# A decoder layer on one core: ScalarE copies products out of PSUM, GpSimd's queue takes late stores, scores and values are put side by side, and round 0 loads by use

## The chip, the cores and the metric

The kernel runs on one core of a Trainium2 chip. TensorE (PE) multiplies matrices into PSUM, VectorE (DVE), ScalarE (ACT) and GpSimd (POOL) work on tiles, and DMAs move data between SBUF and DRAM. DMAs are issued by SyncE (SP), by ACT and, after the change, by POOL; each issues its own instructions in order. The metric is the device time of one execution in microseconds (us), the median of three runs.

## The reference

One decoder layer, with layer normalization behind each of its three parts. `x` is 8 x 512 x 512. In the first part, attention runs over the axis of length 8, for each of the 512 columns by itself, with 16 heads of 32 and relative positions. In the second, each of 8 batches attends from its 512 positions to 512 context vectors of 1024 features, with 8 heads of 64 and a mask. The third is a feed-forward part of width 2048, whose hidden values and second weight are rounded to an 8-bit float.

```python
qkv = x @ in_proj_weight.T + in_proj_bias
ac = einsum('tbhd,sbhd->bhts', q + r_w_bias, k)
bd = rel_shift(einsum('tbhd,rhd->bhtr', q + r_r_bias, p))[..., :t]
ctx = einsum('bhts,sbhd->tbhd', softmax((ac + bd) * scale), v)
x = layernorm(x + ctx @ out_proj_weight.T + out_proj_bias)
...
k, v = split((ctx_2048 @ W_src.T + b_src) * mask)
q = (x @ W_tgt.T + b_tgt) * mask
u = softmax(where(mask == 0, -inf, q k^T / 8)) v
x = layernorm(x + concat([x, u]) @ W_out.T + b_out)
...
h = float_quantize(relu(x @ w1.T + b1), 4, 3)
x = layernorm(x + float_quantize(h @ float_quantize(w2, 4, 3).T + bq, 5, 10))
```

## The kernel before

**Stage one** computes the first part. The 512 columns are cut into four blocks `j` of 128, and each block has eight positions `t`. PE projects queries (`queries_of`, part 0 of `project`, line 224), keys and values from `xt`; the keys and values are copied to SBUF by ACT (lines 244 and 294), and DVE adds the bias to the queries out of PSUM (line 253). DVE multiplies queries with keys and reduces (`pq`, lines 257 and 266: 2.3 us each), weighs the values with the softmax (`weigh`, lines 321 to 337, into `ao`), PE transposes `ao` (`turn_out`), ACT copies the result to `aoT`, and PE multiplies it with the output weight (`put_out`, line 354). DVE adds this to the residual `r` out of PSUM (line 370) and takes the statistics; behind every fourth position comes a square root on ACT (`sd_a`, line 106), four normalizations, and four stores to `x1d` from ACT's queue (line 376). The projections share two PSUM banks (`ps_mm`), the output product has one (`ps_o`).

Beside this runs a filling of PE's time: `context_work` projects the context of batches 0 to 5 to keys and values (products `px`, `py`, `pz`, line 694), `project_context` does the same for batch 6, one piece of 16 matmuls for each of four key blocks (`psk`) and four value blocks (`psv`). ACT evicts each piece to a tile `st` and stores it to `kd` or `vd` from its own queue (lines 179 and 193).

In this stage the order of PE's instructions is that in which the program writes them. A small planner writes it: `slot` gives each position a length (11.2 for scores, 12.4 for values), `must` places what has to come, and `fill` puts context products between. The other engines' order is left to the framework's scheduler.

**Stage two** goes through rounds `t` = 0 to 7, one for a batch. Here the order of PE, DVE, ACT and SP is the order of the program. A round has units `u`: for each of four pairs of heads `c`, two units of two query blocks. A score unit (`scores`, line 1112, `s`) multiplies queries `qT` with keys `kT`; DVE adds the mask and finds the maximum (`nmax`, line 1127), ACT takes the exponential (line 1137), DVE divides (line 1152) and transposes 32 x 32 blocks (line 1160, `pb`). Behind a pair's second unit `move_blocks` issues 16 DMAs that move the blocks to where their transpose has them (`pT`, line 1176); in round 0 half of them are on ACT's queue. `pT` has one buffer, so the moves of a pair follow the values product of the pair before. The values product (`attend`, line 1213, `av`) multiplies `v` with `pT`. The values of batches 0 to 5 are loaded raw and turned by DVE (`raw`, `turn_v`).

Dense work is woven between: in round 0 the `project_context` of batch 7 (eight pieces, with `w_src` and `ct7`; two of them in round 1), later the output projection of the round before (`output_of`: `px` on `x1T`, `pu` on `u`, lines 1248 and 1260), the second feed-forward product of two rounds before (`finish`, line 1417, `fin` and `o`), the queries of the next round (`psq`, line 1091), and the first feed-forward product (`hidden_of`, line 1328, `hx`, `hy`, `hz`) in a form with seven block products, whose weight slabs `w1r` are loaded by `load_w1` into the memory that `w_src` has until then.

`weave` merges the two lists. An attention step comes when its gap is used up and when as many dense steps are behind it as it needs; the gap that follows is its weight x the dense cost left / the weights left. `attention_of` makes the list: in rounds 1 to 7 the odd units from 3 on are a score step of weight 0.5 and then a values step of weight 0.5, which needs `projected`, the end of `output_of`. Each step goes through `run`, which first issues due loads (`later`, counted down in steps) and due moves, and then earns credit (0.7 of the step's cost, 1.3 in round 0) for side work on DVE and ACT: `urgent` (the normalization of `x2`) before `side` (exponentials, divisions, transposes, turns, output stores).

At the start of round 0 SP is given `x1T(1)` (four DMAs), the row `bxo` and `x1(0)` at once, ahead of the dense steps; the stores of batch 7's pieces are put on `later` and issued one step behind. After the normalized `x2` is turned, SP stores it (`x2d`, four DMAs, line 1007) and loads it back whole (`x2T`, line 1014).

Of the kernel before, what the change touches and what calls it, by code (L numbers as in the profile page):

```python
# [9 lines left out]
F32 = mybir.dt.float32  # L10
# [3 lines left out]
ALU = mybir.AluOpType  # L14
# [3 lines left out]
P = 128  # L18
E = 512
EC = E // P  # L20

T, NB, H1, D1 = 8, 512, 16, 32
NJ = NB // P
# [15 lines left out]
R_BQ, R_RW, R_BO, R_BXO, R_B2 = range(5)  # L39
# [3 lines left out]
def decoder_layer(  # L43
# [22 lines left out]
    nc = tc.nc  # L66
# [27 lines left out]
    def load_row(pool, r, name):  # L94
        tl = pool.tile([P, E], F32, name=name)
        nc.sync.dma_start(tl, rows[r].partition_broadcast(P))
        return tl
# [60 lines left out]

    big = ctx.enter_context(tc.tile_pool(name="big", bufs=1))

    def project_context(t, w, ct_of, ps_pool, ps_tag, st_pool, st_tag, store):

        def keys(o):
            ps = ps_pool.tile([P, S], F32, tag=ps_tag, name=f"psk{t}_{o}")
            for f in range(FC):
                nc.tensor.matmul(  # L170
                    ps,
                    lhsT=w[0][f][:, o * P : (o + 1) * P],
                    rhs=ct_of(f),
                    start=(f == 0),
                    stop=(f == FC - 1),
                )
            st = st_pool.tile([P, S], F32, tag=st_tag, name=f"kst{t}_{o}")
            nc.scalar.activation(st, ps, AF.Identity, bias=col(C_BK + o))
            store(lambda: nc.scalar.dma_start(kd[t][:, o, :], st))

        def values(s):
            ps = ps_pool.tile([P, E], F32, tag=ps_tag, name=f"psv{t}_{s}")
            for f in range(FC):
                nc.tensor.matmul(  # L184
                    ps,
                    lhsT=ct_of(f)[:, s * P : (s + 1) * P],
                    rhs=w[1][f],
                    start=(f == 0),
                    stop=(f == FC - 1),
                )  # L190
            st = st_pool.tile([P, E], F32, tag=st_tag, name=f"vst{t}_{s}")
            nc.scalar.activation(st, ps, AF.Copy, scale=maskcol[:, t, s : s + 1])
            store(lambda: nc.scalar.dma_start(vd[t][:, s, :], st))

        return [lambda o=o: keys(o) for o in range(EC)] + [
            lambda s=s: values(s) for s in range(ST)
        ]

    with ExitStack() as ph:
# [46 lines left out]
        def queries_of(j, t):  # L246


            if t == 0:
                sc[j] = kvp.tile([P, T, P], F32, tag="sc", name=f"sc{j}")  # L250
            ps = project(xts[j, t], 0, f"q{j}_{t}")
            qw = qp.tile([P, E], F32, tag="qw", name=f"qw{j}_{t}")
            nc.vector.tensor_tensor(qw, ps, bqw, ALU.add)  # L253
            for g in range(2):
                fs = slice(g * HW, (g + 1) * HW)
                pr = prp.tile([P, HH, T, D1], F32, tag="pr", name=f"pq{j}_{t}_{g}")
                nc.vector.tensor_tensor(  # L257
                    pr,
                    qw[:, fs]
                    .rearrange("p (h d) -> p h d", d=D1)  # L260
                    .unsqueeze(2)
                    .to_broadcast([P, HH, T, D1]),
                    k_all[j][:, :, fs].rearrange("p s (h d) -> p h s d", d=D1),
                    ALU.mult,
                )
                nc.vector.tensor_reduce(  # L266
                    sc[j][:, t, g * HH * T : (g + 1) * HH * T],
                    pr.rearrange("p h s d -> p (h s) d"),
                    AX.X,
                    ALU.add,  # L270
                )
# [79 lines left out]
        def put_out(j, t):  # L351
            po = ps_o.tile([P, E], F32, tag="po", name=f"po{j}_{t}")
            for c in range(EC):
                nc.tensor.matmul(  # L354
                    po,
                    lhsT=aoT[t][:, c * P : (c + 1) * P],
                    rhs=w_o[:, c, :],
                    start=(c == 0),
                    stop=(c == EC - 1),
                )  # L360
            r = rp.tile([P, E], F32, tag="r", name=f"r{j}_{t}")
            n0 = t * NB + j * P
            nc.sync.dma_start(r, x[n0 : n0 + P, :])
            nc.gpsimd.tensor_tensor(r, r, bo, ALU.add)
            if t % 4 == 0:
                normed["mv"] = sm.tile([P, 4, 2], F32, tag="mv1", name=f"mva{j}_{t}")
                normed["r"] = []
            mvs, rts = normed["mv"], normed["r"]
            rts.append(r)
            nc.vector.tensor_tensor(r, po, r, ALU.add)  # L370
            stats_of(sm, mvs[:, t % 4, :], r, f"a{j}_{t}")
            if t % 4 == 3:
                rs = rstd_of(sm, mvs, 4, f"a{j}_{t}")
                for i in range(4):
                    normalize(rts[i], rts[i], mvs, rs, i)
                    nc.scalar.dma_start(x1d[t - 3 + i][j], rts[i])

# [419 lines left out]
        def last_but_one():  # L799
            for f in range(FC):  # L800
                ct6.append(xtp.tile([P, S], F32, tag="xt", name=f"ct6{f}"))
                nc.sync.dma_start(ct6[f], ctxT[T - 2, f * P : (f + 1) * P, :])
            return project_context(
                T - 2, w6, lambda f: ct6[f], ps_kv, "kv", kst, "st", lambda f: f()
            )

        filling.append(context_work())
# [82 lines left out]
    with ExitStack() as ph:  # L890
# [45 lines left out]
        def run(cost, step):  # L936

            nonlocal credit
            move()
            credit += pace * cost  # L940
            while credit > 0 and (urgent or side):
                _, work, f = (urgent or side).pop(0)
                credit -= work
                f()
            credit = min(credit, 0.0)
            step()
# [21 lines left out]
        def load_x1(t):  # L968
            x1[t] = qx.tile([P, NJ, E], F32, tag="x1", bufs=2, name=f"x1{t}")
            nc.sync.dma_start(x1[t], x1d[t].rearrange("j p e -> p j e"))  # L970
# [14 lines left out]
        def load_x1T(t):  # L985
            x1T[t] = x1Ts[:, t % 2]
            load_blocks(x1T[t], x1d[t])
# [475 lines left out]
        def of(cost, f, *a):  # L1463
            return [(cost, lambda: f(*a))]
# [34 lines left out]
        def attention_of(t, projected, queried):  # L1499

            steps = []
            last = t + 1 == T
            behind = 2 if t == 0 else 1
            for u in range(1, 2 * EC + (0 if last else 1)):
                n = units[t * 2 * EC + u]
                need = queried if u == 2 * EC else 0
                values = u > 2 * behind and (u % 2 == 1 or (t == 0 and u == 2 * EC))
                weight = 0.5 if values else 1.0  # L1510
                score = (2.0, need, lambda n=n: scores(*n), weight)
                if not values:
                    steps.append(score)
                    continue
                f = lambda c=u // 2 - behind: attend_next(t, c)

                weight = 2.2 if last and u == 2 * EC - 1 else 0.5
                value = (3.8, projected, f, weight)
                steps += [value, score] if t == 0 else [score, value]
            return steps  # L1520

        def output_of(t):
# [11 lines left out]
        with tc.manual_schedule(engines={ET.PE, ET.DVE, ET.Activation, ET.SP}):  # L1534
# [30 lines left out]
            for t in range(T):  # L1565
# [5 lines left out]
                asked = [of(3.6, queries, t + 1, o, mq) for o in range(EC) if t + 1 < T]  # L1571
                asked = sum(asked, [])
                if t == 0:
                    load_x1T(1)
                    bxo = load_row(wb, R_BXO, "bxo")
                    load_x1(0)

                    pieces = project_context(
                        T - 1,
# [3 lines left out]
                        "b",  # L1583
                        sp,
                        "pe",
                        lambda f: later.append([1, f]),
                    )
                    steps = sum([of(7.2, piece) for piece in pieces[:-2]], []) + asked

                    behind = {  # L1590
                        1: of(0.0, convert, 0) + of(0.0, cast_b2),
                        3: of(0.0, convert, 1) + of(0.0, turn_v_soon, 1),
                        4: of(0.0, turn_x1, 1),
                    }
# [3 lines left out]
                else:  # L1598
# [12 lines left out]
                    sums = [of(0.0, sum_x2, t - 1, i) for i in range(4)]  # L1611
                    if t == 1:
                        dense += x1_ahead + after + done[0] + of(0.0, load_x2T, 0)
                        dense += done[1]
                        for i, part in enumerate(((0, 0), (1, 0), (0, 1))):
                            asked[2 * i + 1 : 2 * i + 1] = of(0.0, load_w1, *part)
                    elif t < T - 1:
                        dense += x1_ahead + done[0] + after
                        dense += done[1] + of(0.0, load_x2T, t - 1)
                    else:  # L1620
                        dense += after + done[0] + done[1]
                        for j in range(2):
                            dense += of(0.9, turn_late_x2, t - 1, j)
# [129 lines left out]
```

## Time and profile before

| what | us |
|---|---|
| median of three runs (lowest to highest) | 2048.33 (2047.96 to 2048.45) |
| the profiled execution | 2051.27 |
| its span | 2049.0 |
| PE busy in the span | 2001.7 |
| stage one, to about 867: PE, DVE, ACT, POOL busy | 849.5, 756.5, 117.5, 122.8 |
| 867 to 1066 (round 0, start of round 1): PE, DVE, ACT busy | 182.2, 135.5, 53.5 |
| one of the repeating rounds (136.4): PE, DVE, ACT busy | 135.5, 96.1, 53.1 |

The page gives busy time by engine. In the list of waits a line names the engine, its instruction and source line, what ended the wait, and then the total, the number and the longest of such waits in us. A timeline line has start and length in us, engine, source line, operation, what is written and read, the shape, how many instructions were merged, and in brackets the idle time before it and its cause. `SPq` and `ACTq` are DMA issues in SP's and ACT's order. In the windows the granted clock of TensorE is given as a share: 1.00 is full speed.

### The profile page before, as it was taken

How to read it: one execution, taken by the hardware profiler on the slowest of the kernel's cores; microseconds unless marked ns; L12 is line 12 of the kernel's file. 1: busy time of each engine (PE TensorE's matmuls, PEld its weight loads, DVE VectorE, ACT ScalarE, POOL GpSimd, SP SyncE). 2: the span in 40 equal slices, each digit the busy share in tenths (PEclk: the TensorE clock that was granted, in tenths of full speed). 3: DMA queues.
4: the chain of work that ended last, by engine and by line, in shares of the span. 5: the costliest groups of instructions: out<-in, count | busy, mean ns of one | idle time of the engine just before them, and what ended most of it. 6: DMA issues, size and time to landing. Idle time of an engine off the chain costs nothing.

```text
span 2049.0 us, 19491 instructions
## 1 busy us (share of the span) xinstructions
PE 2001.7 (98%) x6552; PEld 1040.1 (51%) x6552; DVE 1524.0 (74%) x2409; ACT 547.3 (27%) x1194; POOL 214.7 (10%) x211
## 2 busy tenths in 40 slices
PE   9999999999999999998999999999999999999998
PEld 4544444444444444443347456465474564655666
DVE  4999999999999979348675685775856857657343
ACT  2111101110111011123235244253352442534322
POOL 0040012012102120011001001002010010000000
PEclk9999999999999999999999999999999999999999
DMA  6635235342242541497677566676775666753711
GB/s 222 235 103 212 75 121 197 110 159 79 77 166 76 186 164 72 106 291 195 147 204 214 127 166 219 117 223 163 148 215 120 168 218 133 211 154 93 230 47 66
DMA packets 247075, 319.37 MB, mean 156 GB/s; under 512 B 85056, under 2 KB 140352, under 8 KB 242880
## 3 DMA queue, kind: packets, MB, share of 16 engines
q1 hardware_dynamic: 227040, 283.22, 48.9%
q10 hardware_dynamic: 19936, 34.91, 5.1%
q8 instruction: 52, 0.85, 0.2%
q14 instruction: 47, 0.39, 0.1%
HBM read 188.03 MB, written 62.91 MB: 122 GB/s over the span
## 4 chain that ended last, share of the span: by engine, by line
PE 70%; DVE 22%; issue 3%; DMA 2%; SPq 1%; ACT 1%; POOL 0%; ACTq 0%; DVEq 0%
PE hx L1328 11%; PE pox L1260 6%; PE hz L1328 5%; PE pox L1248 5%; PE s L1112 5%; PE av L1213 5%; PE px L694 5%; PE po L354 4%; DVE sc L266 4%; DVE pq L257 3%; PE ps_q L224 3%; PE psv L184 3%; PE o L1417 3%; PE hy L1328 3%; PE psq L1091 3%
## 5 line engine op out<-in xcount | busy, mean ns | idle before, releaser
L1137 ACT ACTIVATE pe<-pe,nmax 128x512 f32<-128x512 f32 x256 | 182.7, 715 | 265.5 <-DVE nmax L1127 236.1
L1127 DVE CUSTOM_DVE_ANT_0 pe<-s,mb 128x512 f32<-128x512 f32 x256 | 162.6, 683 | 27.7 <-PE s L1112 26.9
L1160 DVE STREAM_TRANSPOSE pb<-pe 128x512 f32<-128x512 f32 x256 | 161.7, 681 | 2.4 <-DMA pT<-pb 2.4
L321 DVE TENSOR_TENSOR pv<-v,sc 128x2048 f32<-128x2048 f32 x64 | 147.0, 2298 | 7.4 <-ACT v L294 5.6
L257 DVE TENSOR_TENSOR pq<-qw,k 128x2048 f32<-128x2048 f32 x64 | 151.1, 2361 | 1.2
L266 DVE TENSOR_REDUCE sc<-pq 128x64 f32<-128x2048 f32 x64 | 145.9, 2280 | 1.1
L1112 PE MATMUL s<-kT,qTx 64*128 64x512 f32 x512 | 130.1, 624 | 9.3 <-DMA kT<-kd 5.7
L354 PE MATMUL po<-w_o,aoT 128*128 128x512 f32 x256 | 117.6, 603 | 5.4 <-DVE r L370 5.4
L1213 PE MATMUL av<-pT,vx 128*64 128x512 f32 x512 | 118.6, 606 | 2.9 <-DMA pT<-pb 2.9
L1328 PE MATMUL hx<-x2T,w1r 128*128 128x256 f32 x512 | 118.6, 382 | 2.0 <-ACT hs L1350 2.0
L1091 PE MATMUL psq<-x1Ts,w_tgt 128*128 128x512 f32 x256 | 115.7, 609 | 4.9 <-DVE x1Ts L983 4.9
L224 PE MATMUL ps_k<-w_in,xt 128*128 128x512 f32 x256 | 116.0, 606 | 4.6 <-DMA xt<-in_xT_dram 4.6
L224 PE MATMUL ps_q<-w_in,xt 128*128 128x512 f32 x256 | 117.0, 600 | 2.7 <-DVE qw L253 2.7
L1328 PE MATMUL hx<-x2s,w1r 128*128 128x256 f32 x512 | 118.6, 382 | 0.8 <-DVE hs L1356 0.8
L1356 DVE TENSOR_TENSOR hs<-hz,hs 128x512 f32<-128x512 f32 x32 | 22.1, 692 | 130.0 <-PE hz L1328 128.3
L1152 DVE TENSOR_SCALAR pe<-pe,rden 128x512 f32<-128x512 f32 x256 | 114.8, 491 | 4.5
L1260 PE MATMUL pox<-w_xo,uT 128*128 128x512 f32 x256 | 115.0, 598 | 0.0
L224 PE MATMUL ps_v<-w_in,xt 128*128 128x512 f32 x256 | 114.4, 593 | 0.1
L1248 PE MATMUL pox<-w_xo,x1Ts 128*128 128x512 f32 x256 | 114.0, 593 | 0.0
L1417 PE MATMUL o<-w2q,hq 128*128 128x512 fp8e4 x512 | 113.6, 379 | 0.0
L1328 PEld LDWEIGHTS hx<-x2s,w1r 128*128 128x128 f32 x512 | 96.0, 190 | 25.1 <-DVE nmax L1127 4.5
L1328 PEld LDWEIGHTS hx<-x2T,w1r 128*128 128x128 f32 x512 | 97.8, 192 | 18.1 <-ACT hs L1350 2.4
(169 smaller groups left out, 2859.7 us busy)
## 6 DMA issues: line engine op xcount, KB each, us to landing
pT<-pb SPq DMA_DIRECT2D x480, 128.0 KB, 2.4
w1r<-w1d SPq DMA_DIRECT2D x32, 1024.0 KB, 6.6
w1r<-w1d SPq DMA_DIRECT2D x32, 768.0 KB, 4.6
ch<-in_ctxT_dram SPq DMA_DIRECT2D x24, 512.0 KB, 6.1
td<-tx SPq DMA_DIRECT2D x12, 768.0 KB, 4.9
tx<-td SPq DMA_DIRECT2D x12, 768.0 KB, 7.5
r<-in_x_dram SPq DMA_DIRECT2D x32, 256.0 KB, 4.1
x1d<-r ACTq DMA_DIRECT2D x32, 256.0 KB, 2.5
```

What stands on the lines that cost most here:

```text
L224: nc.tensor.matmul(ps, lhsT=xt[:, e, :], rhs=w_in[:, e, part * E : (part + 1) * E], start=(e == 0), stop=(e == EC - 1),)
L257: nc.vector.tensor_tensor(pr, qw[:, fs] .rearrange("p (h d) -> p h d", d=D1) .unsqueeze(2) .to_broadcast([P, HH, T, D1]), k_all[j][:, :, f ...
L266: nc.vector.tensor_reduce(sc[j][:, t, g * HH * T : (g + 1) * HH * T], pr.rearrange("p h s d -> p (h s) d"), AX.X, ALU.add,)
L354: nc.tensor.matmul(po, lhsT=aoT[t][:, c * P : (c + 1) * P], rhs=w_o[:, c, :], start=(c == 0), stop=(c == EC - 1),)
L1091: nc.tensor.matmul(ps, lhsT=w_tgt[:, e, o * P : (o + 1) * P], rhs=x1T[t][:, e, :], start=(e == 0), stop=(e == EC - 1),)
L1112: nc.tensor.matmul(ps[:, h, :], lhsT=qT[t, c][half[h], j * P : (j + 1) * P], rhs=kT[t, c][half[h], :], start=True, stop=True,)
L1137: nc.scalar.activation(pe, pe, AF.Exp, bias=nmax[:, h : h + 1], scale=-1.0, accum_out=den[:, h : h + 1],)
L1213: nc.tensor.matmul(av[half[h], :], lhsT=v[t, c][:, s, half[h]], rhs=pT[t, c][:, :, :, s, h].rearrange("p g i q -> p (g i) q"), start=(s == 0),
L1248: nc.tensor.matmul(po, lhsT=x1T[t][:, e, j * P : (j + 1) * P], rhs=w_xo[:, e, :], start=(e == 0), stop=False,)
L1260: nc.tensor.matmul(po, lhsT=uT[t][:, e, j * P : (j + 1) * P], rhs=w_xo[:, EC + e, :], start=False, stop=(e == EC - 1),)
L1328: nc.tensor.matmul(banks[g, name][:, i], lhsT=w[:, f, i * P : (i + 1) * P], rhs=b[:, f], start=start and f + i == 0, stop=f == 1, skip_gro ...
L1417: nc.tensor.matmul(po, lhsT=rows_of_j, rhs=w2q[:, c, :], start=(c == 0), stop=(c == HC - 1),)
```

## The change

Five edits are made together.

- In `queries_of` and `put_out` ACT copies the product from PSUM to SBUF (to `qw`, and over `aoT[t]`, which the product has read), and DVE adds from SBUF.
- `project_context` issues its stores from POOL's queue, for both batches, and at once; the delay for batch 7 goes. The last four stores of `x1d` (block 3, positions 4 to 7) are also issued by POOL.
- In rounds 1 to 6 the odd units from 3 on are one step of weight 1.0, which holds the scores and, through a `run` of its own, the values product; it needs what either needed.
- In round 0 `x1T(1)` is loaded behind the first dense step, and `bxo` and `x1(0)` behind the third.
- In round 1 `load_w1(0, 0)` goes ahead of the transposes of `x1T` and the queries; the two that follow go one step later among the queries.

```diff
             st = st_pool.tile([P, S], F32, tag=st_tag, name=f"kst{t}_{o}")
             nc.scalar.activation(st, ps, AF.Identity, bias=col(C_BK + o))
-            store(lambda: nc.scalar.dma_start(kd[t][:, o, :], st))
+            nc.gpsimd.dma_start(kd[t][:, o, :], st)
...
             nc.scalar.activation(st, ps, AF.Copy, scale=maskcol[:, t, s : s + 1])
-            store(lambda: nc.scalar.dma_start(vd[t][:, s, :], st))
+            nc.gpsimd.dma_start(vd[t][:, s, :], st)
...
             qw = qp.tile([P, E], F32, tag="qw", name=f"qw{j}_{t}")
-            nc.vector.tensor_tensor(qw, ps, bqw, ALU.add)
+            nc.scalar.copy(qw, ps)
+            nc.vector.tensor_tensor(qw, qw, bqw, ALU.add)
...
-            nc.vector.tensor_tensor(r, po, r, ALU.add)
+            nc.scalar.copy(aoT[t], po)
+            nc.vector.tensor_tensor(r, aoT[t], r, ALU.add)
...
-                    nc.scalar.dma_start(x1d[t - 3 + i][j], rts[i])
+                    queue = nc.gpsimd if j == NJ - 1 and t == T - 1 else nc.scalar
+                    queue.dma_start(x1d[t - 3 + i][j], rts[i])
...
-                value = (3.8, projected, f, weight)
-                steps += [value, score] if t == 0 else [score, value]
+                if t == 0 or last:
+                    value = (3.8, projected, f, weight)
+                    steps += [value, score] if t == 0 else [score, value]
+                    continue
+
+                def both(n=n, f=f):
+                    scores(*n)
+                    run(3.8, f)
+
+                steps.append((2.0, max(need, projected), both, 1.0))
...
-                    load_x1T(1)
-                    bxo = load_row(wb, R_BXO, "bxo")
-                    load_x1(0)
+                    bxo = wb.tile([P, E], F32, name="bxo")
+
+                    def load_rows():
+                        nc.sync.dma_start(bxo, rows[R_BXO].partition_broadcast(P))
+                        load_x1(0)
...
-                        lambda f: later.append([1, f]),
...
                     behind = {
+                        0: of(0.0, load_x1T, 1),
                         1: of(0.0, convert, 0) + of(0.0, cast_b2),
+                        2: of(0.0, load_rows),
...
-                        dense += done[1]
-                        for i, part in enumerate(((0, 0), (1, 0), (0, 1))):
-                            asked[2 * i + 1 : 2 * i + 1] = of(0.0, load_w1, *part)
+                        dense += done[1] + of(0.0, load_w1, 0, 0)
+                        for i, part in enumerate(((1, 0), (0, 1))):
+                            asked[2 * i + 2 : 2 * i + 2] = of(0.0, load_w1, *part)
```

More of the change, by code (lines that the diff above doesn't have):

```diff
@@ L159, in decoder_layer, with project_context @@
     big = ctx.enter_context(tc.tile_pool(name="big", bufs=1))
-    def project_context(t, w, ct_of, ps_pool, ps_tag, st_pool, st_tag, store):
+    def project_context(t, w, ct_of, ps_pool, ps_tag, st_pool, st_tag):
         def keys(o):
@@ L803, in last_but_one @@
             return project_context(
-                T - 2, w6, lambda f: ct6[f], ps_kv, "kv", kst, "st", lambda f: f()
+                T - 2, w6, lambda f: ct6[f], ps_kv, "kv", kst, "st"
             )
```

## The prediction

> **What bounds the kernel now.** I read the table of busy time first, then PE's waits, then short windows around the long waits, and last the timeline of one repeating round.
>
> ```profile
> span 2049.0 us, 19491 instructions
> PE 2001.7 (98%) x6552; PEld 1040.1 (51%) x6552; DVE 1524.0 (74%) x2409; ACT 547.3 (27%) x1194; POOL 214.7 (10%) x211
> ```
>
> PE is idle for 47.3 us only, and the change takes no matmul away. So it can win PE's idle time, the slow clock behind it, and the cost of switching between kinds of matmul; nothing else. The list of PE's waits says where the idle time lies:
>
> ```profile
> PE s L1112 <- DMA kT<-kd: 5.7, 1, 5.7
> PE po L354 <- DVE r L370: 5.4, 2, 4.4
> PE psq L1091 <- DVE x1Ts L983: 4.9, 1, 4.9
> PE s L1112 <- DVE nmax L1127: 3.6, 4, 0.9
> PE hy L1328 <- DMA w1r<-w1d: 3.5, 1, 3.5
> PE av L1213 <- DMA pT<-pb: 2.9, 1, 2.9
> PE ps_q L224 <- DVE qw L253: 2.7, 1, 2.7
> ```
>
> The change aims at four of these lines: po, ps_q, s on kT, hy on w1r. Windows cut just behind the ends of such waits show a second price (columns: PE, PEld, DVE, ACT, POOL busy, then the granted clock):
>
> ```profile
> 425.60:432.00 6.40, 6.31 (x12) 2.93 (x13) 4.12 (x7) 0.00 (x0) 0.00 (x0) 0.62 0.94 350
> 490.80:496.10 5.30, 5.27 (x9) 2.25 (x10) 5.30 (x5) 0.21 (x1) 0.00 (x0) 0.68 0.00 0
> 930.20:937.00 6.80, 6.76 (x13) 2.67 (x14) 4.40 (x8) 0.61 (x2) 1.48 (x2) 0.60 0.87 218
> 1199.00:1203.00 4.00, 3.11 (x12) 1.28 (x12) 3.89 (x11) 2.08 (x6) 0.00 (x0) 1.00 0.94 204
> ```
>
> After waits of 4.43, 2.72 and 5.74 us the clock is 0.60 to 0.68 for some 5 to 7 us; after one of 0.89 us it stays 1.00. A long wait thus costs 1.8 to 2.9 us more.
>
> In the second stage I read round 2 (PE, then SP's DMA queue):
>
> ```profile
> 1163.80 1.99 PE L1112 MATMUL s<-kT,qTx 64*128 64x512 f32 x8
> 1165.72 7.08 PE L1417 MATMUL o<-w2q,hq 128*128 128x512 fp8e4 x32
> 1172.73 3.65 PE L1213 MATMUL av<-pT,vx 128*64 128x512 f32 x16
> ...
> 1201.20 1.13 PE L1112 MATMUL s<-kT,qTx 64*128 64x512 f32 x4 [0.89 <-DVE nmax L1127]
> ...
> 1209.36 3.65 PE L1213 MATMUL av<-pT,vx 128*64 128x512 f32 x16
> ```
>
> ```profile
> 1180.23 3.54 SPq L1007 DMA_DIRECT2D x2d<-x2T  x4
> 1187.42 0.38 SPq L1014 DMA_DIRECT2D x2T<-x2d  x1
> 1194.52 10.26 SPq L1176 DMA_DIRECT2D pT<-pb  x16
> ```
>
> The values product `av` needs the block transposes' DMAs `pT`. For the second pair of heads these end on SP at 1204.8; with 2.4 us to landing they are there at 1207, and `av` starts at 1209.4: only 2 us to spare.
>
> **The change part by part.**
>
> *ScalarE copies (`queries_of`, `put_out`).* 64 copies are added, at 586 ns each (the same copy of `k`, `v`, `aoT`): 37.5 us on ACT, busy 117 us of the first stage's 867. DVE's 64 additions stay; they take 676 and 684 ns from PSUM now, and 688 to 692 with both inputs in SBUF (`tx`, `x`): +0.8 us, hidden where DVE waits for PE. The gain is that PE's bank is free after ACT's copy. At 421.1 to 425.7 PE waited 4.43 us for `po`; with ACT free, the `aoT` and `po` copies follow one another and leave about 0.4: 4.0 gained, and 2.4 of slow clock (the `po` group took 6.04 us, usually 3.60). Next late is DVE: the two transposes of `ao` after it have 4.4 and 3.0 us of slack now, and DVE itself comes 2.3 us earlier; I give back 1.2. The `ps_q` wait is worth 2.7 and 1.8 of clock, but ACT is in order: from 476.7 to 490.2 it stood before the square root `sd_a`, waiting for DVE, with a copy of `v` behind it. If the `q` copy is queued behind it too, the wait stays. I count 3.0 of 4.5. At the stage's end the copy lengthens PE, DVE, ACT, DVE to `psq` (4.9 us) by 0.6, and 0.2 comes back at the previous `po`. Sum: 7.5 gained; bounds 0 (DVE, over 95% busy in most windows, holds PE) and 11.
>
> *Stores in GpSimd's queue.* 16 stores of keys and values and the last 4 of `x1d` leave ACT's queue, where one issue takes 0.33 to 0.45 us; the delayed ones are no longer delayed. No row shows a DMA issued by POOL. From below the price is ACT's 0.33; from above, 1.4 us, as for ACT's eight `pT` issues beside a busy SP (11.5 us). It matters at one place: SP waits 9.1 us for `x1d<-r` before `kT`, the mask, `w_src` and `ct7`, and POOL's own mask work is then behind the four issues. `ct7c`, issued at 883.8 with 7.9 to landing, is used at 893.96: 2.2 us to spare. So I take 0, and keep +3 for the range (four issues 1.4 apart, less the spare time). Without the 2.2 us, PE's first `psk` would wait. The Trainium skill ("SBUF — State Buffer", section "A bandwidth-pool intuition that's wrong (but worth ruling out)") speaks against it: GpSimd can't write a DMA's descriptors while DVE's op holds their shared port, and a DMA of 620 ns took 3100 so. No row here shows it; by it the first store would land 2.5 us later, and the sum would be 0.3 us worse.
>
> *Loads of round 0.* `x1T(1)` (4 DMAs) now goes behind `raw` (4) and `kT`, and ahead of the first `pT` half (8); `bxo` and `x1(0)` (2) behind the next `kT` and the first `w2f`. Now SP blocks 11.3 us on the second `x1T`, and `kT` is issued at 926.56. After: near 900, so the 5.74 us and 2.7 of clock lose their cause. Next late: ACT issues its eight `pT` from 906.7 to 918.2, its exponentials wait, DVE frees the score bank near 927.3 where PE wants it at 924.5. I leave 2.8 plus 1.2 of clock: 4.4 gained; bounds 0 (ACT's issues blocked longer beside the later `x1T`) and 8.4. For round 1, `load_w1(0,0)` moves ahead of the 16 `pT` issues (1045.96 to 1058.2) behind which it stood; it can go once PE is through with `w_src` at 1041.9, and lands by 1052: the 3.5 us and 2.9 of clock go. The other two slabs go one step later, issued after the `pT`, wanted 6 us behind that: nothing.
>
> *Scores and values side by side.* In rounds 1 to 6 three `av` follow their scores directly. A group behind `s` or `av` takes 0.1 to 0.2 us longer (`pox` x8: 3.63 against 3.43). 18 switches less by 0.15: 2.7; bounds 0 and 3.6. But every `av` comes earlier. The planner sets a gap of weight x dense cost left / weights left. Round 2 has 112.6 of dense cost and weight 8: odd scores stand at 38.4, 75.8 and 110.6, their `av` at 48.0, 85.0 and 119.8. Now they stand at the scores; only the last two move, by 1.8. The first has its `pT` at 1158.4 and needs it at 1165.7: safe. The third: landing 1231.4, wanted near 1235: safe. The second is not. Credit for side work comes earlier too, so the order on SP becomes `x2d`, `x2T`, `pT`, `out`. Walked through with the rows: `av` at 1165.7 pushes the two `fin` products by 3.6; DVE's four normalizations and transposes end at 1183.5 (now 1180.2); `x2d` to `x2T` takes 7.2 as now: 1190.7; `pT` from 1191.1, 10.26 of issue, landing near 1203.5. PE comes to it at 1201.0. A new wait of 2.45 us, in each of rounds 2 to 6; the 0.9 before it (rounds 2 to 5) goes, since `exp` comes earlier. The bounds: 0 and 3.5 a round. Waits of 2.3 to 2.9 us were followed by a slow clock, the one of 2.0 at 1887 was not; I take 0.7 of 1.75. Loss: 5 x 3.15 - 3.6 = 12.2. In round 1 the same `pT` lands near 1060.7 with PE there at 1059.2, and the first one 0.5 late: 3.2 of the 6.4 stay gained (bounds -1 and 6.4).
>
> The Trainium skill ("TensorE: Matmul & The Clock Gate", section "What's actually happening") halves the clock after an idle window of 3.4 us. Our 2.9 us wait already did it. By the page 2.45 us would cost no clock: 3.5 us better.
>
> **Sum.** -7.5 + 0 - 4.4 - 3.2 - 2.7 + 12.2 = -5.6 us. The profiled execution took 2051.27 us (span 2049.0 and 2.3 around it), 2.9 over the median of 2048.33; I take the difference off the median: about 2042.5.
>
> **Rivals.**
> 1. *The `pT` are in time.* If DVE's turn ends 2.5 us earlier than I walked, the new waits vanish and only gains are left: 17.8 + 3.6, so 2027. For it: `pT` is free of the `out` store. Against it: the 7.2 from `x2d` to `x2T` is fixed.
> 2. *The new wait decides; slower.* `pT` 1 us later and the full 1.75 of clock each time: 5 x 5.2 - 3.6 = 22.4 lost against 17.8: 2053. It decides from 4.3 us a round on (21.4 / 5). For it: the slow clock after 2.7 and 2.9. Against: each round is alike, so one lucky phase spares all.
> 3. *The banks are freed, but the first stage gains nothing*, as DVE is the next bound or the `q` copy stands behind `sd_a`: 7.5 less, 2050. For it: DVE's windows of 24 to 25 us in 25. Against: from 725 to 750 DVE is busy 14.9 of 25, waiting for PE.
>
> **How the numbers follow.** Forecast 0.42, rivals 0.20, 0.22, 0.16. The sum's uncertainty is about 6 us, so the forecast's own range is 2036 to 2049. The range goes from 2 us below rival 1 to 5 above rival 2, whose waits may reach the upper bounds: 2025 to 2058. A measurement here tells 0.2%, 4 us: faster is below 2044.2, with 0.26 of the forecast, rival 1 and 0.04 of rival 3: 0.50; same 0.24; slower 0.26.
>
> **What would show it.** Right: `po <- DVE r`, `ps_q <- DVE qw` and `hy <- w1r` gone from PE's waits, `s <- kT` gone or turned into `s <- nmax` under 4 us, and `av <- pT` up from 1 wait to 5 or more of 2 to 3 us. Wrong: `av <- pT` still at one (then rival 1), PE waiting on ACT copies in the first stage, or `psq` and `psk` waiting longer for loads behind POOL's stores.

## The result, and the profile after

The changed kernel takes 2068.39 us (median of 4 runs, 2065.15 to 2073.78), the kernel before 2048.39 beside it. The ratio is 1.0095, with a 95% interval of 1.0069 to 1.0122: 14 to 25 us slower. The forecast was 2042.5, its range ended at 2058. The profiled execution took 2067.04 us, 1.4 below its median, and that of the kernel before 2.9 above its own; so the two profiles lie only 16.2 us apart. The head of the page:

```profile
span 2065.2 us, 19573 instructions
PE 1999.4 (97%) x6552; PEld 1040.3 (50%) x6552; DVE 1534.0 (74%) x2409; ACT 570.3 (28%) x1248; POOL 228.2 (11%) x231
```

PE is busy 2.3 us less than before and idle 18.5 us more (65.8 us, before 47.3); the span has grown by 16.2. PE's waits in the changed kernel (from the copies on its source lines are up to 3 higher than before):

```profile
PE psq L1094 <- DVE x1Ts L986: 20.6, 6, 5.6
PE px L697 <- DVE st L739: 5.8, 4, 3.2
PE s L1115 <- DVE nmax L1130: 5.3, 2, 5.0
...
PE ps_q L224 <- ACT qw L253: 3.9, 2, 3.2
PE av L1216 <- DMA raw<-vd: 3.4, 1, 3.4
PE ps_v L224 <- ACT v L295: 3.0, 2, 2.1
PE av L1216 <- DMA pT<-pb: 2.8, 1, 2.8
```

The lines that the change aimed at are gone: `po <- DVE r`, `ps_q <- DVE qw`, `s <- kT`, `hy <- w1r`. But each has a successor, and the first line is new in kind. In the kernel before, the queries `psq` waited once for their transposed input `x1Ts`, 4.9 us at the end of stage one. Now they wait six times. The forecast named `av <- pT` in rounds 2 to 6 as the new wait; it is listed once, and that is in round 1, at 1062.

The starts of the first `psq` and of the first `pox` in a round, read off PE's timeline, cut the run into stretches. They tell where the time went:

| stretch | before, us | after, us | difference |
|---|---|---|---|
| start to the last `po` | 866.7 | 868.5 | +1.8 |
| to the first `psq` (end of stage one) | 4.9 | 5.6 | +0.7 |
| round 0, to the `psq` inside it | 82.7 | 80.9 | -1.8 |
| to the `psq` of round 1 | 89.3 | 88.6 | -0.7 |
| to the first `pox` of round 2 | 82.8 | 79.0 | -3.8 |
| rounds 2 to 6 | 680.8 | 701.1 | +20.3 |
| the rest, to PE's last matmul | 235.1 | 235.1 | 0 |

Rounds 2 to 6 lose 3.6 to 4.7 us each. The smaller differences are near the scatter of single executions: the runs below whose first stage is as before end it between 864.3 and 866.4, and those whose round 0 is as before take 168.9 to 172.7 from the first `psq` to that of round 1, where the kernel before took 172.1 and the changed one 169.6. Here is one of the losing rounds, round 2, in PE's timeline of the changed kernel (start, length, group; in brackets the idle time before it and its cause):

```profile
1159.91 1.99 PE L1115 MATMUL s<-kT,qTx 64*128 64x512 f32 x8
1161.83 3.65 PE L1216 MATMUL av<-pT,vx 128*64 128x512 f32 x16
1165.42 13.99 PE L1420 MATMUL o<-w2q,hq 128*128 128x512 fp8e4 x64
1179.34 1.99 PE L1115 MATMUL s<-kT,qTx 64*128 64x512 f32 x8
1181.26 1.98 PE L1094 MATMUL psq<-x1Ts,w_tgt 128*128 128x512 f32 x4
1186.25 13.98 PE L1094 MATMUL psq<-x1Ts,w_tgt 128*128 128x512 f32 x28 [3.01 <-DVE x1Ts L986]
1200.16 1.99 PE L1115 MATMUL s<-kT,qTx 64*128 64x512 f32 x8
1202.55 3.65 PE L1216 MATMUL av<-pT,vx 128*64 128x512 f32 x16 [0.41 <-issue]
```

And the same product in the kernel before:

```profile
1185.25 14.00 PE L1091 MATMUL psq<-x1Ts,w_tgt 128*128 128x512 f32 x32
```

Before, 32 matmuls run through in 14.0 us. After, four run, PE stands for 3.01 us, and the other 28 take 13.98 instead of 12.25 (28 x 14.00/32): 1.7 us of slow clock. The granted clock behind the wait, in windows of the changed kernel (window; its length; PE, PEld, DVE, ACT, POOL busy; the clock; then the DMA share and GB/s):

```profile
1186.25:1192.00 5.75, 5.75 (x10) 2.49 (x11) 5.24 (x10) 0.30 (x1) 1.04 (x1) 0.70 0.65 199
1192.00:1200.00 8.00, 8.00 (x20) 3.33 (x18) 7.89 (x21) 4.22 (x9) 0.00 (x0) 1.00 1.05 227
```

Why chunk 2 of the input is late stands in DVE's timeline. Before, from the first pair of chunks to the second:

```profile
1180.06 1.26 DVE L983 STREAM_TRANSPOSE x1Ts<-x1Ts 128x512 f32<-128x512 f32 x2
...
1182.81 0.68 DVE L1425 TENSOR_TENSOR o<-o,b2q 128x512 f16<-128x512 f32 x1
...
1185.09 1.27 DVE L983 STREAM_TRANSPOSE x1Ts<-x1Ts 128x512 f32<-128x512 f32 x2
```

After:

```profile
1179.72 1.26 DVE L986 STREAM_TRANSPOSE x1Ts<-x1Ts 128x512 f32<-128x512 f32 x2
1180.91 2.44 DVE L1163 STREAM_TRANSPOSE pb<-pe 128x512 f32<-128x512 f32 x4
1183.28 0.65 DVE L1428 TENSOR_TENSOR o<-o,b2q 128x512 f16<-128x512 f32 x1
...
1185.51 1.27 DVE L986 STREAM_TRANSPOSE x1Ts<-x1Ts 128x512 f32<-128x512 f32 x2
```

DVE ends the second pair 0.4 us later than before by these clocks, but PE has come 4.0 us sooner (`psq` at 1181.26, before 1185.25). That PE came out of round 1 sooner is not the cause, since rounds 3 to 6, which follow rounds as slow as themselves, show the same 3.0 us. The cause lies within the round. Counted from the scores `s` ahead of the output products (1163.80 before, 1159.91 after), `psq` comes 0.1 us sooner, the first turn on DVE 3.6 us later and the second 4.3 later. For `av` now stands ahead of all four output products `o`, where two of them stood ahead of it; those two, and on DVE what follows their `finish` in order, come 3.6 us later, and the pair's block transposes `pb` (2.44 us) have come ahead of the second turn. This was the theory for the experiments, called Q below: **query chunks late**.

### The profile page after: what moved, and what is told of

Read it like the earlier page. It is cut to its first block, busy times and chain, and to the rows that moved or that the text cites. A ratio compares the mean times of both kernels' runs of the same rounds, so it can differ in the third digit from the quotient of the medians.

```text
span 2065.2 us, 19573 instructions
## 1 busy us (share of the span) xinstructions
PE 1999.4 (97%) x6552; PEld 1040.3 (50%) x6552; DVE 1534.0 (74%) x2409; ACT 570.3 (28%) x1248; POOL 228.2 (11%) x231
## 4 chain that ended last, share of the span: by engine, by line
PE 69%; DVE 22%; DMA 3%; issue 3%; ACT 1%; SPq 1%; POOL 0%; ACTq 0%; DVEq 0%; POOLq 0%
PE hx L1331 11%; PE pox L1263 5%; PE pox L1251 5%; PE hz L1331 5%; PE av L1216 5%; PE px L697 5%; PE s L1115 4%; PE po L355 4%; PE ps_q L224 3%; DVE sc L267 3%; PE ps_v L224 3%; DVE pq L258 3%; PE psq L1094 3%; PE hy L1331 3%; PE ps_k L224 2%
## 5 line engine op out<-in xcount | busy, mean ns | idle before, releaser
L1094 PE MATMUL psq<-x1Ts,w_tgt 128*128 128x512 f32 x256 | 125.5, 648 | 20.6 <-DVE x1Ts L986 20.6
L1359 DVE TENSOR_TENSOR hs<-hx,hs 128x512 f32<-128x512 f32 x64 | 44.0, 687 | 94.2 <-PE hx L1331 94.2
L1331 PEld LDWEIGHTS hx<-x2T,w1r 128*128 128x128 f32 x512 | 95.5, 190 | 30.8 <-issue 16.2
```

Source lines behind the costliest of these rows:

```text
L1094: nc.tensor.matmul(ps, lhsT=w_tgt[:, e, o * P : (o + 1) * P], rhs=x1T[t][:, e, :], start=(e == 0), stop=(e == EC - 1),)
L1331: nc.tensor.matmul(banks[g, name][:, i], lhsT=w[:, f, i * P : (i + 1) * P], rhs=b[:, f], start=start and f + i == 0, stop=f == 1, skip_gro ...
```

## The experiments

All times are medians; each ratio is against runs of the kernel before on the same chip (medians 2049.0 to 2049.3). A stretch or a wait is read from one profiled execution of each run.

| run | what it is | us | ratio, 95% |
|---|---|---|---|
| e1 | before + side by side | 2065.1 | 1.0088 (1.0072 to 1.0103) |
| e2 | changed, without side by side | 2049.5 | 1.0002 (0.9993 to 1.0010) |
| e3 | before + both ScalarE copies | 2052.6 | 1.0018 (1.0009 to 1.0028) |
| e4 | changed, all query chunks turned at once | 2085.5 | 1.0181 (1.0168 to 1.0194) |
| e5 | before + moved loads | 2041.9 | 0.9967 (0.9955 to 0.9980) |
| e6 | before + stores on GpSimd | 2046.5 | 0.9989 (0.9980 to 0.9997) |
| e7 | before + side by side, first pair only | 2067.5 | 1.0094 (1.0079 to 1.0110) |
| e8 | before + side by side, second pair only | 2078.1 | 1.0145 (1.0131 to 1.0159) |
| e9 | e5 + value stores on GpSimd | 2039.0 | 0.9959 (0.9945 to 0.9972) |
| e10 | e9 + side by side, third pair only | 2038.2 | 0.9945 (0.9933 to 0.9957) |
| e11 | before + copy of `po` | 2049.8 | 1.0001 (0.9993 to 1.0010) |
| e12 | before + copy of `ps_q` | 2054.0 | 1.0026 (1.0016 to 1.0036) |

**Which part loses: e1 and e2.** e1 is the kernel before with the edit of `attention_of` alone; e2 is the changed kernel with that edit undone.

```diff
-                value = (3.8, projected, f, weight)
-                steps += [value, score] if t == 0 else [score, value]
+                if t == 0 or last:
...
+                def both(n=n, f=f):
+                    scores(*n)
+                    run(3.8, f)
+
+                steps.append((2.0, max(need, projected), both, 1.0))
```

> The kernel before with one edit: scores and values side by side in rounds 1 to 6. Theory Q (query chunks late): with the values ahead of the two last output products, DVE comes to the copies of query chunks 2 and 3 only after the pair's block transposes; the first query product psq waits about 3 us in each of rounds 2 to 6 and the clock drops behind it, 4 us a round in all. Then this kernel alone is 16 to 20 us slower than before, 2064 to 2068 us, with psq <- x1Ts five waits near 3 us each. Rival E (elsewhere): the loss of 20 us comes from the copies, the stores and the moved loads; then this kernel is within 5 us of 2048, and its list of waits has no psq <- x1Ts beyond the 4.9 us at the start.

> The changed kernel without the side by side edit: copies, stores and moved loads stay. Theory Q: the waits of psq in rounds 2 to 6 are gone and the time is 2045 to 2051 us: about 2 us lost by the end of the first stage (waits on ACT and DVE there, kT later), 0 to 5 us won by the loads. Rival E: 2060 us or more.

Measured 2065.1 and 2049.5: the edit alone costs 1.0088, all the others together cost nothing. In e1 `psq` waits as in the changed kernel, in e2 only at the end of stage one:

```profile
PE psq L1091 <- DVE x1Ts L983: 20.0, 6, 4.9
```

```profile
PE psq L1094 <- DVE x1Ts L986: 5.6, 1, 5.6
```

The rival E falls. Side by side is the loss; whether Q is its mechanism needed two more steps.

**Is it only where the chunks are turned: e4.** In the changed kernel the second pair of chunks is turned with the first, ahead of the last two `finish`:

```diff
-                        dense += of(0.0, turn_x1, t + 1, 0, 1)
+                        dense += of(0.0, turn_x1, t + 1)
                     dense += done[2]
-                    if t + 1 < T:
-                        dense += of(0.0, turn_x1, t + 1, 2, 3)
-                    else:
+                    if t + 1 == T:
```

> The changed kernel with all four query chunks copied ahead of the last two outputs' finish, in place of two ahead and two behind. Theory Q: the 3 us waits of psq in rounds 2 to 6 go (to under 1 us each), 8 to 20 us less than the changed kernel: 2048 to 2060. If the block transposes' transfers are the next late (as the prediction had it), av <- pT shows 2 to 3 us in four or five rounds and the time is at the upper end, 2056 to 2062; if not, the lower end, 2046 to 2052. Rival S: side by side costs 4 us a round by itself (switches, slow clock, DVE's load), wherever the chunks are copied: then the time stays at 2064 to 2070.

Theory and rival both missed: 2085.5, slower still. Its list of waits:

```profile
PE av L1216 <- DMA out_dram<-x: 20.5, 4, 5.2
PE av L1216 <- DMA pT<-pb: 9.9, 2, 5.1
```

and `psq` waits once only, 5.6 us at the end of stage one. So the long waits of `psq` are gone, as Q said, and PE runs on to the next late thing: the values product of the second pair, whose transposes are still on SP. The line names an output store in four of six, where that store's event comes last in the profile; SP's order in e4 shows that the 16 `pT` stand right before it:

```profile
1193.49 11.86 SPq L1179 DMA_DIRECT2D pT<-pb  x16
1205.44 2.11 SPq L1443 DMA_DIRECT2D out_dram<-x  x4
```

`av` starts at 1208.91, 3.6 us behind the last `pT` issue; PE had stood for 5.22 us. The transposes are slow to land, too. From issue to landing (shortest, median, longest) the `pT` of this round take, in the kernel before and in e4:

```profile
DMA to landing us min/median/max: 2.3/2.4/2.5
```

```profile
DMA to landing us min/median/max: 3.9/4.6/6.8
```

In e4, as in the changed kernel (3.5, 4.5, 6.9), they are issued right behind the load of `x2T`; before, 6.7 us behind it. So Q explains the wait at `psq`, and not the whole loss: behind that wait stands a longer one.

**Which pair does which: e7 and e8.** The edit of e1 for one of the three pairs each:

```diff
-                if t == 0 or last:
+                if t == 0 or last or u != 3:
```

and `u != 5` in e8.

> The kernel before with scores and values side by side for the first of the three pairs of each round only (unit 3). Theory Q: it is this values product, ahead of the last two output products, that puts the query chunks late: psq <- x1Ts waits 3 us in each of rounds 2 to 6, 12 to 17 us slower than before, 2061 to 2066. Rival P, the prediction's: the values product of the second pair, which comes to its transposes too early, decides; then this kernel is within 3 us of before.

> The kernel before with scores and values side by side for the second of the three pairs only (unit 5). Theory Q: no psq wait in rounds 2 to 6; av waits 0 to 1 us for pT: 2046 to 2052. Rival P: av waits 2 to 3 us in each of rounds 2 to 6, 10 us or more above before: 2058 to 2064.

Both are slower, e8 by more than either theory had: each was right about its own pair and wrong in denying the other's. With the first pair alone `psq` waits (its line in e7, the same as in e1), with the second alone `av` (its lines in e8):

```profile
PE psq L1091 <- DVE x1Ts L983: 20.0, 6, 4.9
```

```profile
PE av L1213 <- DMA pT<-pb: 22.9, 6, 4.7
PE av L1213 <- DMA out_dram<-x: 4.7, 1, 4.7
```

The second pair is the dearer, 29 us against 18, though the changed kernel has both and loses 20. The two don't add up, because both are waits for one chain on DVE and SP; whoever waits first gives the later one its time, as e4 shows by taking the first wait away. In the changed kernel `psq` waits 3.0 us and loses 1.7 of clock, and `av` then waits 0.41 us (the row names no cause, but the last `pT` lands about then), 0.2 to 1.0 in the other rounds. In e8 the transposes start 9.3 us behind `psq`, as in the kernel before, where the changed kernel has 6.1; only `av` asks for them sooner. SP's order in e8:

```profile
1182.51 0.38 SPq L1014 DMA_DIRECT2D x2T<-x2d  x1
1189.19 0.36 SPq L1440 DMA_DIRECT2D out_dram<-x  x1
1189.64 10.25 SPq L1176 DMA_DIRECT2D pT<-pb  x16
```

As in the kernel before, the first output store stands ahead of `pT`. It waits for a normalization that DVE ends at 1189.2, while the block transposes were done at 1187.1: 2 us of SP's order, in the same round in which `av` waits 4.48.

**The copies: e3, e11, e12.** The two edits of `queries_of` and `put_out`, together and one by one.

```diff
-            nc.vector.tensor_tensor(qw, ps, bqw, ALU.add)
+            nc.scalar.copy(qw, ps)
+            nc.vector.tensor_tensor(qw, qw, bqw, ALU.add)
...
-            nc.vector.tensor_tensor(r, po, r, ALU.add)
+            nc.scalar.copy(aoT[t], po)
+            nc.vector.tensor_tensor(r, aoT[t], r, ALU.add)
```

> The kernel before with the 64 ScalarE copies alone. The prediction's step 1 said 7.5 us gained (2041). Theory A (ACT in order): the copy of a query product and of an output product stand in ACT's queue behind the square root that waits for DVE, so po <- DVE and ps_q <- DVE are replaced by ps_q, ps_v <- ACT and px <- DVE st of about the same length: 2047 to 2051, and the end of the first stage moves by less than 2.5 us either way. Rival D: DVE is the bound of the first stage's windows and the copies only lengthen its chain to psq: 2050 to 2054, with the first psq 2 or more us later than before.

> The kernel before with the ScalarE copy of the output products alone. By the prediction's step 1: 4.0 and 2.4 won at po, 1.2 given back: 5.2 less, 2043. Theory D (DVE paces the first stage; what PE gains it waits for at the next place where it needs DVE): po's 4.4 us go, px <- DVE st and ps_q <- DVE qw grow by about as much; 2047 to 2051.

> The kernel before with the ScalarE copy of the query products alone. By the prediction's step 1: 3.0 won, 0.6 lost at the end of the first stage: 2046. Theory A (ACT in order): the copy stands in ACT's queue behind the square root that waits for DVE; ps_q <- DVE 2.7 turns into ps_q or ps_v <- ACT of 2 to 5 us in all, 2049 to 2053; the waits of px at 174 and 372 stay as they were before if the output copies made them longer.

The copy of `po` is worth nothing (1.0001), the copy of `ps_q` costs 3 to 7 us, both together cost 2 to 6. e3 has the waits that theory A named (`px`, `ps_q`, `ps_v`) and the time of theory D. In e11 the wait of 4.43 us at `po` is gone, and PE waits 5.21 at `ps_q` (before 2.72):

```profile
PE ps_q L224 <- DVE qw L253: 5.2, 1, 5.2
```

This is as theory D has it: DVE paces this stage, and what PE gains it waits for at the next place. In e12 ACT's group of these copies reads (idle time before them at the end, by cause):

```profile
L253 ACT COPY qw<-ps_q 128x512 f32<-128x512 f32 x32 | 18.8, 586 | 165.9 <-PE ps_q L224 105.1 <-DVE pq L258 39.5 <-DVE st L737 12.6
```

The copy's target `qw` has two buffers, and the one it wants can still be read by an earlier product `pq` on DVE; five of the waits before these 32 copies, 39.5 us together, are ended by that. There the copy doesn't free PE's bank when ACT is free, but when DVE is, and ACT's other copies stand behind it. The square root `sd_a`, which I had suspected, isn't what holds them: near 490 one of these copies runs ahead of it and the next 5 us behind, when `pq` ends. A wait of `px` near 372 is 1.45 us with this copy alone, 0.44 in e11 and absent before, so it is for the most part not the output copies' doing. A third buffer for `qw` wasn't tried: that the held buffer is the price is read from the trace, not shown by taking it away.

**Loads and stores: e5, e6, e9.** e5 has the two load edits of rounds 0 and 1, e6 the stores. In e9 the value stores alone are added to e5:

```diff
-            store(lambda: nc.scalar.dma_start(vd[t][:, s, :], st))
+            nc.gpsimd.dma_start(vd[t][:, s, :], st)
```

> The kernel before with the moved loads of rounds 0 and 1 alone. By the prediction's step 3: the wait of s on kT (5.7 and 2.7 of slow clock) shrinks to 2.8 and 1.2, and hy on w1r (3.5 and 2.9) goes: 10.8 less, 2038. Theory N: in round 0 the maximum of the scores (nmax) is late by itself, because ACT's eight issues of pT hold the exponentials; then s <- kT turns into s <- nmax of 5 to 6 us as with the changed kernel, only the w1r part is won: 2042 to 2044. Theory G: the stores from GpSimd make nmax late; then here, without them, s <- nmax is at most 3 us.

> The kernel before with the stores moved to GpSimd's queue alone. By the prediction's step 2: 0, or up to 3 us more: 2048 to 2052. If the stores of x1d come late by 1.7 us as in the changed kernel (kT issued 7.4 us behind the last output product, before 5.7), psk waits about 1 us for ct7c, and the first store of keys waits in POOL's order behind the mask work and holds ACT. Theory G for round 0: s waits 6 us or more (kT or nmax), 0 to 2 us above before. Rival: the stores free ACT and win 1 to 2 us: 2046 to 2048.

> The kernel before with the moved loads, and of the stores only the eight of the values of the batches 6 and 7 (four each) from GpSimd's queue; the keys stay in ACT's. Theory G: what made the stores harmful to the moved loads is the first store of keys, which stands in POOL's order behind the mask work; the values' stores come later and stand behind nothing long. Then round 0 is as with the loads alone (no long wait of s), the wait of hy for w1r may shrink: 2038 to 2042. Rival: any store by GpSimd takes the gain of round 0 away, 2045 or more.

All three are faster than before, by 0.1 to 0.4%. In e5 the stretch of round 0 up to its `psq` falls from 82.7 to 74.5 us, without any wait of `s` there; in the changed kernel it was 80.9, with a wait of 4.98 for `nmax`. What stands between is in POOL's order of the changed kernel:

```profile
912.08 1.93 POOL L967 TENSOR_SCALAR mb<-mq 128x512 f32<-128x512 f32 x1 [26.62 <-DMA mq<-in_mask_dram]
914.09 1.50 POOL L968 TENSOR_SCALAR mq<-mq 128x512 f32<-128x512 f32 x1
915.53 0.61 POOL L179 DMA_DIRECT2D kd<-kst  x1
```

and in ACT's:

```profile
918.34 0.69 ACT L178 ACTIVATE kst<-psk,colv 128x512 f32<-128x512 f32 x1 [13.44 <-DMA kd<-kst]
918.50 5.79 ACTq L1179 DMA_DIRECT2D pT<-pb  x8
```

The first key piece is in `kst` at 900.85, but its store stands behind the mask work for the next batch, which waits until 912, and is issued at 915.53, 14.7 us after the piece is ready. ACT's next piece wants a buffer that this store still holds, so ACT stands 13.44 us with its eight `pT` behind it. In e5 ACT issues them at 908.68:

```profile
908.68 5.51 ACTq L1176 DMA_DIRECT2D pT<-pb  x8
```

Theory G holds, and e9, where only the keys' stores stay with ACT, keeps the gain of round 0 (74.8 us to `psq`). What e5 wins is 8.2 us up to that `psq`, of which 4.2 go again before the `psq` of round 1 (a new `s <- nmax` of 2.1 at 951 and some 1.8 of slow clock behind it; the wait of `av` there is 3.2 on `raw` for 2.9 on `pT` before), and 3.4 in round 1, where `w1r` still costs 2.7: 7.4 in all, as the times have it.

e6 loses in round 0 (`s` on `kT` 8.44, before 5.74) and wins in round 1: no wait of `hy` is left over 0.2 us, as SP issues the 16 `pT` ahead of `w1r` in 10.5 us instead of 12.25 and PE comes 1.9 us later; 6.1 us less up to the first `pox` of round 2. In e2 that stretch wins 6.3, not more, so what the two edits win there is one and the same wait, and in round 0 the one spoils the other's gain. With 2 to 6 us for the copies on top, nothing is left of 7.4 and 2.8 in e2, by the medians. This sum is an account from rows; no run has the loads and all stores without the copies.

**A better version: e10.** The third pair side by side (`u != 7`) on top of e9.

> The kernel of the run before this one, with scores and values side by side for the third pair (unit 7) of rounds 1 to 6. Theory Q: the third pair's values have nothing late behind them, neither query chunks nor transposes; six or twelve switches fewer win 1 to 2 us against the run before: 2037 to 2041. Rival P: its transposes come late as the second pair's do: 4 us a round more, 2055 or more.

2038.2 us, 0.9945 of the kernel before, the fastest of all. Each of rounds 2 to 6 is 0.2 us shorter than in e9, as the starts of two `psq` show, 136.39 us apart in e9 and 136.20 in e10:

```profile
1445.60 14.00 PE L1091 MATMUL psq<-x1Ts,w_tgt 128*128 128x512 f32 x32
1581.99 14.00 PE L1091 MATMUL psq<-x1Ts,w_tgt 128*128 128x512 f32 x32
```

```profile
1446.72 14.00 PE L1091 MATMUL psq<-x1Ts,w_tgt 128*128 128x512 f32 x32
1582.92 14.00 PE L1091 MATMUL psq<-x1Ts,w_tgt 128*128 128x512 f32 x32
```

This fits the price that the forecast had put on the fewer switches. The intervals of e9 and e10 overlap, so the step between them is read from the rounds, not from the times.

## Why the prediction was wrong

The forecast and all three rivals miss: the cause of the loss was in none of them. Rival 2 had the direction, but by a wait at another place and with 2053. (The recorded expectations number the prediction's parts: 1 copies, 2 stores, 3 loads, 4 side by side.)

- *Step 4, side by side* failed, at the walk of round 2. It put the new wait at `av <- pT`, by following the delayed `fin` products to the normalizations, to `x2d`, `x2T` and `pT`. It noted that DVE's work is pushed by 3.6 us and didn't ask what else is queued in it: the second turn of `x1`, whose reader `psq` stands earlier in PE's order than `av`. The slack was readable: in DVE's timeline of before the second turn copies chunk 2 from 1185.1 to about 1185.7, and `psq` asks for that chunk after four of its 32 matmuls, near 1187.0. About 1.3 us was there; the turn came 4.3 us later in the round, and 3.0 is the difference. So the wait came in each of rounds 2 to 6: 3.0, mostly 1.7 of clock and 0.2 to 1.0 at `av`, less the 0.9 of `nmax` (which round 6 didn't have before) and, as the remainder, 0.2 to 0.5 of switching. The five rounds lost 20.3, where the step had 12.2 less 2.7.
- The mechanism that the step did name exists, and was undersized. It had `pT` start 5.85 us behind `psq`; in the changed kernel and in e4 this is 6.1. But the 16 issues, which follow at once on the load of `x2T`, took 11.9 us in e4, not 10.26, and `av` could start 3.6 us behind the last of them, where the step had about 2.1. With the wait at `psq` removed, PE waits 5.2 us (e4), not 2.45. Rival 2 was this wait with 1 us more; the changed kernel isn't its case, because the wait that it is made of was 0.41.
- One pair side by side, one switch less a round by the step's count, saved 0.2 a round (e10), where the step had 0.15: as sized.
- *Step 1, the copies*, failed: 7.5 gained was forecast, bounds 0 to 11, measured 2 to 6 lost. The bound at 0 was wrong, since an engine put between PE and DVE can lose. The `po` term (5.2) was 0 as PE only waited later, which rival 3 had priced; the `ps_q` term had the wrong sign, by the trace of e12 because the copy needs a buffer that DVE holds. The step's own terms add up to 7.8, not 7.5. The term of the stage's end, 0.6, was right: the wait of the first `psq` is 5.57 for 4.90.
- *Step 2, the stores*: 0, up to +3, measured -4 to -1 alone. The place named (`ct7c`) costs 0.9 us in e2, 0.4 in e6, and no wait in the changed kernel. The costly place was another, the key store behind the mask work. "POOL's own mask work is then behind the four issues" looked at what waits behind the stores and not at what the stores wait behind.
- *Step 3, the loads*, was right in kind. With the loads alone (e5) round 0 wins 4.0 net, where the step had 4.4, though by another way, so the match is luck: 8.2 first, nearly the upper bound, with ACT's eight `pT` issues at 5.5 us where the step went by the 11.5 of before, and 4.2 given back later in the round. Round 1 wins 3.4 where the step had 6.4 without side by side. In the changed kernel round 0 wins 2.5, within the scatter, for the store of step 2 stands in the way; round 1 wins 3.8 up to the first `pox` of round 2, for 3.2 foretold. But e1, without any moved load, wins 5.7 in that stretch, so these 3.8 aren't shown to be the loads'.

Of the signs set out beforehand, the four waits did go; reading only whether they go would have passed the change. What decides is the table of stretches.

The prediction weighed two rules of the Trainium skill. From "SBUF — State Buffer", section "A bandwidth-pool intuition that's wrong (but worth ruling out)", it took that a DMA of GpSimd can take 3100 ns where 620 is usual, while DVE holds the shared port. In no issue here does that show: the 20 issues by POOL took 0.56 to 0.59 us each on the mean, the longest 0.74, beside a DVE busy for 74% of the span, and the key and value stores landed 2.8 and 3.2 us after issue (medians), where ACT's took 2.5. The danger of that queue was its order. From "TensorE: Matmul & The Clock Gate", section "What's actually happening", it took that the clock is halved after an idle window of 3.4 us. Waits of 3.0 us were followed by slow clock (28 matmuls in 13.8 us or more) in 13 of 15 rounds (2 to 6 of the changed kernel, e1 and e7), and by none in the two others (12.28 us). Elsewhere a wait of 3.36 us (`av` at 981 in the changed kernel) cost no clock, and one of 2.90 (`av` at 979 before) did, 5.35 us for 3.65. Over all 14 traces, every wait of 3.5 us or more was followed by slow clock, and about half of those of 1.9 to 3.4 us. So the rule's length is no safe lower bound here, and the same wait isn't always punished.

## What to carry to other kernels

When PE's work is moved ahead by some microseconds, list every consumer on the engine that gets its input later, in the order in which PE will ask for them, and compare each with its slack: the first that fails sets the cost, and hides the ones behind it. A copy by an idle engine frees a bank only once its target buffer is free too. A store moved to a quiet queue inherits what that queue waits for, and while it waits it holds its source tile.

## What the runs showed of the hardware

A DMA issue by POOL takes 0.56 to 0.59 us on the mean, by ACT mostly 0.33 us for the same store (one took 1.51). Sixteen transposing moves on SP's queue take 10.2 to 10.5 us of issue when they start 3.8 to 7.0 us behind the load of `x2T` with no slab of `w1r` in between, and 11.4 to 12.5 right behind it; in the rounds read above they then land 3.5 us or more after issue, where 2.4 is the median before. Three microseconds of idle PE ahead of `psq` cost 1.5 to 1.7 us of clock in 12 cases of 15, 3.0 in one and none in two; from 3.5 us on, every wait cost some.
